# The row-sum test and its second path at the program's end, attention by halves of the channels, and the first convolution tile prepared in the last attention unit

## The chip, the cores and the metric

The kernel runs on one core of a Trainium2 chip. The metric is the device time of one execution in microseconds (us). PE is TensorE (matmuls), DVE is VectorE, ACT is ScalarE, POOL is GpSimd; SP issues most of the loads, ACT and POOL issue the stores. A core has 16 DMA engines which serve all of these queues. PSUM is the buffer into which matmuls write, in banks of 128 x 512 fp32 numbers.

## The reference

A network of four layers on x of 4 images x 256 channels x 64 x 64, each as x + layer(groupnorm(x)) with 32 groups. Only the first two layers and the start of the third matter here:

```
x = x + _L0(_gn(x))      # attention along each image row, 16 groups
x = x + _L1(_gn(x))      # 3x3 convolution with ternary weights
x = x + _L2(_gn(x))      # two grouped 3x3 convolutions of signs, batch norms
x = x + _L3(_gn(x))      # 3x3 convolution with computed weights

# _L0, for each image row n and group g:
qkv = batchnorm(einsum('nci,oc->noi', x, w_qkv));  q, k, v = split(qkv)
qe = einsum('ngci,cij->ngij', q, q_emb);  ke = the same with k, k_emb
qk = einsum('ngki,ngkj->ngij', qe, ke)
sim = softmax(sum of batchnorm([qk, qe, ke]), over j)
attn   = einsum('ngij,ngcj->ngci', sim, v)       # "values"
attn_e = einsum('ngij,cij->ngci', sim, v_emb)    # "embedded"
out = batchnorm([attn, attn_e]) summed in pairs  # the third batch norm
```

The softmax subtracts the row's maximum. The kernel first computes it without the subtraction, notes whether all row sums stay between 1e-20 and 1e20, and has a second path with the subtraction in case they do not. With these inputs they do, and the second path does not run.

## The kernel before

The whole program is one stream of instructions per engine. Most of the order on each engine comes from the order of the program text; a scheduler may move instructions, except where `tc.high_priority()` raises a block or `tc.keep_in_program_order` pins one. Buffers come from pools: a pool's slots are reused, and an instruction that writes a reused slot waits for the last reader of it. Pools grow from the left or the right side of the memory (`side="right"`).

The stages by the trace: normalisation and qkv product up to 285 us; scores qk into the DRAM buffer qk_d up to 970 (L471 to L599); attention up to 1558; the ternary convolution "d" in Winograd form from 1586 to 2111 (L1000, tiles named dc); the two binary convolutions, "e" (L1237, tiles pc), up to 2407; the last convolution "g" (L1000 again, tiles gc) up to 2941; then the last output store.

**Attention** works in 8 units (b, th): image b and half th of the channels, ordered with th inside b. A unit has 8 steps k of its scores: `scores` loads 1 MB of qk into one of three buffers si (L746) and a q tile (qc, L725, scaled on ACT at L734), makes the relative term by matmul (L757) and adds both on DVE into pt (L767); `exponentials` run on ACT (L797); `sums` are matmuls into den (L808). `reciprocals` inverts den on DVE (L817), lets POOL multiply the range test into the tile `good` (L821, L822), and spreads the result through PE and ACT to rb (L826, L828). Then come 8 `values` (L835) with `values_out` (product with rb L844, bn_stats L849, 256 KB store to at_d[0] by ACT's queue L850, two buffers o0), and 8 `embedded` (L859, product L865) into one 2 MB tile o1, with `next_scores` of the next unit after each. `embedded_out` ends the unit with 8 bn_stats (L874) and one 2 MB store to at_d[1] (L875).

The last unit stops after its reciprocals. Then comes the test: minimum of good over the row (L923), scaling (L924), a matmul (L926), a cast to an integer (L928), and a branch that every engine reads (L930). Behind it `last_unit` does the embedded part first, then the values.

**The norm of the attention's output** is `value_norm(th, two)` (L938 to L957): bn_aggr over the statistics of all images, a square root on ACT (L102, which needs another table than the exponentials), some operations on single columns, a small matmul (L955, pprm).

**Convolution d**: `prepare(b, t)` builds a tile of 128 channels t of the input: `load_1` loads x (dx<-in_x), then for two = 1 and then 0 and 8 pieces each loads a piece of at_d[two] (128 x 512, two issues on SP per piece, two buffers a per value of two) and adds it scaled to x on DVE (L1174); on the second pass DVE takes bn_stats of the sum (L1178). `norm` finds the group norm (matmuls pst, L111 to L122, square root, L1092 and L1181), `transform(b, t, h)` scales half an image on ACT into a padded tile (L1114, L1118) and makes 12 DVE operations of Winograd's input transform (L975 to L986, tile dtr). `rest` runs the 16 chunks (b, h, co): 36 matmuls each into six PSUM banks out of a ring of seven, then the output transform on DVE (L1020 to L1035), the store of x. For the first chunk, `first` = (0, 1): all products of t=0 are made before those of t=1. In program order the first tile is prepared so:

```
set_up()
with tc.high_priority():
    prepare(0, 0)
for t in range(2):
    load_weights(t, nc.sync)
norm(0, slice(0, 1))
transform(0, 0, 0)
prepare(0, 1)
norm(0, slice(1, 2))
transform(0, 1, 0)
for t in range(2):
    transform(0, t, 1)
rest()
```

Of the kernel before, what the change touches and what calls it, by code (L numbers as in the profile page):

```python
# [9 lines left out]
F32 = mybir.dt.float32  # L10
# [7 lines left out]
P = 128  # L18
B = 4
# [21 lines left out]
def network(ctx: ExitStack, tc, x, wqkv, relm, relt, relw, relv, counts, masks, vecs, rowv, ab, w1, l2w1, l2w2, l3w, mats, out):  # L41
# [15 lines left out]
    qk_d = [scratch(f"qk_d{b}", [GP, P, HW]) for b in range(B)]  # L57
    at_d = [[scratch(f"at_d{two}{b}", [C, HW]) for b in range(B)] for two in range(2)]
# [39 lines left out]
    def inv_std(pool, var, eps, shape):  # L98

        t = small(pool, shape)  # L100
        nc.vector.tensor_scalar(t, var, eps, None, ALU.add)
        nc.scalar.activation(t, t, AF.Sqrt)  # L102
        r = small(pool, shape)
        nc.vector.reciprocal(r, t)
        return r
# [560 lines left out]
    cph = ctx.enter_context(ExitStack())  # L666
    cp = pool(cph, "c", side="right")
    st3 = cp.tile([P, 2, 2, B * NB, 6], F32, name="st3")
    qp, ip = cqp, cip
    rp = pool(cph, "c_r")  # L670
    pp = pool(cph, "c_p")
    op = pool(cph, "c_o")
    cp_ = pool(cph, "c_e")
    wp = pool(cph, "c_w", 2)
    pse = pool(cph, "c_pse", 2, PSUM)
    psn = pool(cph, "c_psn", 1, PSUM)
    pso = pool(cph, "c_pso", 3, PSUM)

    vb = [rp.tile([P, 2, 4, 32, 8], F32, name=f"vb{m}") for m in range(4)]
    for m in range(4):  # L680
        nc.gpsimd.memset(vb[m], 0.0)

    pt = pp.tile([P, 32, 4 * 64 * 2 + 16], F32, name="pt")[:, :, 0 : 4 * 64 * 2].rearrange(
        "p i (a n b) -> p i a n b", a=4, b=2
    )
    rb = pp.tile([P, 32, 64, 2], F32, name="rb")

    rw = cp_.tile([P, 127, 2], F32, name="rw")
    nc.sync.dma_start(out=rw, in_=relw)

    ve = cp_.tile([P, W, 32], F32, name="ve")
    nc.gpsimd.memset(ve, 0.0)
    for r in range(2):
        src = bass.AP(tensor=relv.tensor, offset=relv.offset, ap=[[16, 64], [16, 64], [1, 16]])
        nc.sync.dma_start(out=ve[r:P:2, :, 16 * r : 16 * r + 16], in_=src)
    cnt = cp_.tile([P, 16, 32 + P], F32, name="cnt")
    nc.sync.dma_start(out=cnt, in_=counts)
    ones, pick = cnt[:, :, 0:32], cnt[:, :, 32 : 32 + P]
    units = [(b, th) for b in range(B) for th in range(2)]

    def attention(general, good):

        scale_e = se if general else seq

        def load_values(u, m):
            b, th = units[u]
            for r in range(2):
                for h in range(2):  # L710
                    nc.sync.dma_start(
                        out=vb[m][r:P:2, h, :, 16 * r : 16 * r + 16, :]
                        .rearrange("p a c m -> p a (c m)"),
                        in_=vt_d[b][m, r, 64 * h : 64 * h + 64, 4 * th : 4 * th + 4]
                        .rearrange("p a c m -> p a (c m)"),
                    )

        qts = {}

        def terms(u, m):  # L720

            b, th = units[u]
            q = qp.tile([P, 4, 2, 2, 64], F32, name=f"qc_{b}_{th}_{m}_{general}", tag="qc")
            for par in range(2):
                nc.sync.dma_start(  # L725
                    out=q[:, :, par].rearrange("p a k n -> p a (k n)"),
                    in_=q_d[b].rearrange("a (two k) t r c f -> two (k t r c) a f", two=2)[par][
                        :, 4 * th : 4 * th + 4, bass.ts(m, P)
                    ],
                )  # L730
            for a in range(4):
                gp = 4 * th + a
                qf = q[:, a].rearrange("p x k n -> p (x k n)")
                nc.scalar.activation(  # L734
                    qf, qf, AF.Identity, bias=scale_e[:, 1, gp : gp + 1], scale=scale_e[:, 0, gp : gp + 1]
                )
            qts[u, m] = q

        def scores(u, k):

            b, th = units[u]
            if k % 2 == 0:
                terms(u, k // 2)
            q = qts[u, k // 2]
            si = ip.tile([P, 4, 4, P], F32, name=f"si_{b}_{th}_{k}_{general}", tag="si")
            nc.sync.dma_start(  # L746
                out=si.rearrange("p a i f -> p a (i f)"),
                in_=qk_d[b][4 * th : 4 * th + 4].rearrange("a p f -> p a f")[:, :, bass.ts(k, 512)],
            )
            es = [  # L750
                pse.tile([P, 2, 4, 64, 2], F32, name=f"e_{b}_{th}_{k}_{y}_{general}", tag="e") for y in range(2)
            ]
            for par in range(2):
                for x_ in range(4):
                    rows = slice(32 * x_, 32 * x_ + 32)
                    i = 8 * k + 2 * x_ + par
# [4 lines left out]
            for y in range(2):  # L761
# [4 lines left out]
                if not general:  # L766
                    nc.vector.tensor_tensor(dst, e, src, ALU.add)  # L767
                    continue
# [874 lines left out]
```

## Time and profile before

| | |
|---|---|
| time, median of 3 runs | 2950.59 us (2935.45 to 2956.39) |
| the profiled execution | 2953.15 us, its span 2951.4 us |
| PE busy | 2599.9 us, 88% of the span |
| DVE busy | 2063.2 us, 70% |
| ACT busy | 1040.3 us, 35% |
| DMA, mean | 164 GB/s |
| an ordinary attention unit | about 71 us |
| cast of the count, next PE matmul | 1507.24, 1512.14 us |
| last values product ready, first dc matmul | 1558.45 (its DVE product), 1586.05 us |
| dc matmuls without a gap from | 1625.90 us |
| last output store issued, end of span | 2943.53, 2951.4 us |

A line of the timeline has the start and the duration in us, the engine, the line of the kernel, the operation, what it writes and reads, how many instructions are drawn together, and in brackets the idle time of the engine before it and what ended that. "<-issue" means that the profile shows nothing that the engine waited for. The table of stretches gives the busy time of each engine between two times, then the mean clock granted to PE (1 is full), the mean busy share of the DMA engines and what they moved in GB/s.

### The profile page before, as it was taken

What the parts mean: (1) busy time and instruction counts of PE and PEld (TensorE: products, weight loads), DVE (VectorE), ACT (ScalarE), POOL (GpSimd) and SP (SyncE); (2) the same over time, 40 slices, a digit from 0 to 9 for tenths busy, and PEclk for the clock granted to TensorE, in tenths of its full rate; (3) what the DMA queues carried; (4) which work ended last, traced back from release to release, by engine and by line L of the source; (5) the groups of instructions that cost most, each with busy time, mean ns of one, the idle gap of its engine ahead of it and who ended that gap; (6) DMA issues with size and microseconds to landing.
All of it is one profiled execution on the core that took longest, in us unless ns stands there. A gap on an engine that the chain in (4) does not pass through costs nothing. (4 is left out here: it accounts for less than half of the span.)

```text
span 2951.4 us, 77589 instructions
## 1 busy us (share of the span) xinstructions
PE 2599.9 (88%) x34248; PEld 1592.9 (54%) x34248; DVE 2063.2 (70%) x3653; ACT 1040.3 (35%) x1993; POOL 79.3 (3%) x153
## 2 busy tenths in 40 slices
PE   7999889899899787778763999999996978999998
PEld 4666556677677566666652444444454533444443
DVE  6555997666666465556557898985788978859642
ACT  4554445555455644445420010111246821101100
POOL 0000000000000100000000000000000000000000
PEclk9999999999999799988986999999998988999999
DMA  6767465555454777778747435322335663333201
GB/s 236 261 212 218 134 190 141 140 142 134 118 137 101 224 246 242 245 242 265 238 171 236 143 100 176 116 93 94 118 129 196 246 251 114 118 132 111 89 29 43
DMA packets 246806, 484.64 MB, mean 164 GB/s; under 512 B 28672, under 2 KB 128640, under 8 KB 220608
## 3 DMA queue, kind: packets, MB, share of 16 engines
q1 hardware_dynamic: 182304, 294.13, 31.1%
q10 hardware_dynamic: 54880, 125.84, 15.1%
q0 software_dynamic: 9280, 59.64, 5.1%
q8 instruction: 271, 4.44, 0.6%
q14 instruction: 71, 0.58, 0.1%
HBM read 283.20 MB, written 196.35 MB: 162 GB/s over the span
## 5 line engine op out<-in xcount | busy, mean ns | idle before, releaser
L1000 PE MATMUL dc<-dtr,d_u 128*128 128x512 f32 x1152 | 504.2, 598 | 16.9 <-DVE dtr L986 11.5
L1000 PE MATMUL gc<-gtr,g_u 128*128 128x512 f32 x1152 | 505.2, 600 | 14.8 <-DVE pc_o L1249 10.2
L478 DVE STREAM_TRANSPOSE t<-pd 128x1024 f32<-128x1024 f32 x256 | 304.0, 1226 | 113.9 <-PE pd L471 113.9
L1000 PEld LDWEIGHTS gc<-gtr,g_u 128*128 128x128 f32 x1152 | 219.8, 192 | 291.4 <-issue 271.4
L1000 PEld LDWEIGHTS dc<-dtr,d_u 128*128 128x128 f32 x1152 | 218.1, 191 | 287.4 <-issue 264.6
L471 PE MATMUL pd<-rm,qb 64*32 64x256 f32 x8192 | 286.4, 387 | 49.9 <-DVE t L478 43.0
L490 PEld LDWEIGHTS pq<-t,t 64*64 64x64 f32 x8192 | 260.1, 136 | 72.7 <-issue 49.8
L490 PE MATMUL pq<-t,t 64*64 64x64 f32 x8192 | 279.9, 221 | 18.6 <-issue 16.9
L1237 PE MATMUL pc<-e_tr,e_k 128*64 128x512 bf16 x2304 | 260.0, 385 | 19.0 <-DVE e_tr L1227 14.9
L494 ACT ACTIVATE o<-pq 128x512 f32<-128x512 f32 x256 | 152.4, 596 | 320.1 <-PE pq L490 320.0
L797 ACT ACTIVATE pt<-pt,sm 128x512 f32<-128x512 f32 x256 | 163.0, 709 | 198.2 <-DVE pt L767 198.1
L471 PEld LDWEIGHTS pd<-rm,qb 64*32 64x32 f32 x8192 | 156.4, 108 | 135.1 <-DVE t L478 61.9
L1237 PEld LDWEIGHTS <-e_k 128*64 128x64 bf16 x2304 | 141.2, 110 | 134.3 <-issue 21.5
L767 DVE TENSOR_TENSOR pt<-e_False,si_False 128x1024 f32<-128x1024 f32 x128 | 151.5, 1218 | 38.9 <-PE e_False L757 37.8
L499 ACT ACTIVATE pq<-pq 128x512 f32<-128x512 f32 x256 | 149.8, 585 | 3.9
L757 PE MATMUL e_False<-qc_False,rw 32*128 32x256 f32 x1024 | 124.5, 470 | 22.8 <-DVE pt L767 14.2
L1018 ACT COPY gc_c<-gc 128x512 f32<-128x512 f32 x32 | 18.6, 581 | 335.5 <-PE gc L1000 335.5
L835 PE MATMUL pa_False<-pt,vb 128*32 128x64 f32 x4096 | 101.8, 244 | 35.2 <-issue 22.0
L1018 ACT COPY dc_c<-dc 128x512 f32<-128x512 f32 x32 | 18.6, 582 | 321.2 <-PE dc L1000 306.3
L279 PE MATMUL po<-xg,wt 128*128 128x512 f32 x256 | 121.2, 613 | 7.1 <-DVE st L286 5.5
L859 PE MATMUL pe_False<-pt,ve 128*32 128x64 f32 x4096 | 88.8, 239 | 40.9 <-issue 29.8
L294 PE MATMUL pv<-wt,xg 128*128 128x256 f32 x512 | 122.2, 388 | 0.0
(395 smaller groups left out, 3371.1 us busy)
## 6 DMA issues: line engine op xcount, KB each, us to landing
si_False<-qk_d SPq DMA_DIRECT2D x64, 1024.0 KB
qk_d<-o ACTq DMA_DIRECT2D x124, 512.0 KB
x<-x_d SPq DMA_DIRECT2D x32, 1056.0 KB
a<-at_d SPq DMA_DIRECT2D x256, 128.0 KB
xa<-in_x SPq DMA_DIRECT2D x16, 1024.0 KB
vt_d<-vs ACTq DMA_DIRECT2D x32, 512.0 KB
q_d<-qs SPq DMA_DIRECT2D x64, 256.0 KB
qb<-q_d SPq DMA_DIRECT2D x128, 128.0 KB
```

The source lines that it names most:

```text
L279: nc.tensor.matmul(psf, lhsT=wt[:, t, bass.ts(o, P)], rhs=xg[:, t, :], start=(t == 0), stop=(t == 1))
L294: nc.tensor.matmul(pv[:, j, :], lhsT=xg[:, t, pix], rhs=wt[:, t, C : 2 * C], start=(t == 0), stop=(t == 1),)
L471: nc.tensor.matmul(pds[t][32 * c : 32 * c + 32, m].rearrange("p j k -> p (j k)"), lhsT=q[rows, 2 * (gp % 2) + g, a, 32 * nb : 32 * nb + 32 ...
L478: nc.vector.transpose(ts[t][:, :, 32 * jh : 32 * jh + 32].rearrange("p a j b -> p j a b"), pds[t].rearrange("p m j k -> p j m k"),)
L490: nc.tensor.matmul(ps[rows, m, :], lhsT=ts[1][rows, n // 2, :, n % 2], rhs=ts[0][rows, n // 2, :, n % 2], start=True, stop=True, tile_posi ...
L494: nc.scalar.activation(o[:, :, 8 * k : 8 * k + 8, :], ps.rearrange("p n (a b) -> p a n b", b=2), AF.Copy, accum_out=acc[:, 0, gp, col : co ...
L499: nc.scalar.activation(psf, psf, AF.Square, accum_out=acc[:, 1, gp, col : col + 1])
L757: nc.tensor.matmul(es[x_ // 2][:, x_ % 2, :, :, par], lhsT=rw[rows, 63 - i : 127 - i].rearrange("p j r -> p (j r)"), rhs=q[rows, :, par, k ...
L767: nc.vector.tensor_tensor(dst, e, src, ALU.add)
L797: nc.scalar.activation(s, s, AF.Exp, scale=s2q[:, gp : gp + 1])
L1000: nc.tensor.matmul(ms[k], lhsT=u[:, t, dx, k, bass.ts(co, P)], rhs=vs[t][:, k, :, dx : dx + 64], start=(first and dx == 0), stop=(last and ...
L1237: nc.tensor.matmul(m[64 * g : 64 * g + 64], lhsT=parts[:, g, i, k, dx, :], rhs=vs[g][:, k, 8 * (q % 2) : 8 * (q % 2) + 8, dx : dx + 64], s ...
```

## The change

All that follows the scores becomes a function `from_scores(general, keep)`, and the second path is a second call of it: the minimum of `good` is kept in `bad`, and the test (scaling, matmul, cast, branch) stands after the last convolution; if it fails, everything from the attention on is computed once more.

The units run with b inside th, so that th=0 is done for all images after the fourth unit; its two value norms are computed in the fifth (`u == B`), with a PSUM tile of the pool pso. The last unit runs like the others, values and then embedded.

The embedded output leaves in quarters: o1 is 128 x 1024 in two buffers, and after each odd k two bn_stats and a 512 KB store follow. at_d[1] is stored in the quarters' order, and `load_1` reads it by strided views. `load_1` now takes two = 0 first; its a buffers alternate by q (four in all); for image 0 the sum comes from the add itself (accum_out) and the sum of squares from an ACT Square into the spare padded tile, with `whole_stats` to finish, while for the other images four bn_stats follow each half.

The order of the first tile's preparation changes, the weights of d are two tiles loaded at different places, the pools of d, e and g are laid out anew (for d the ring of seven PSUM banks is four banks and three banks of two pools), the row-sum matmul takes its ones as a window of a smaller constant, and `inv_std` takes max(., 0) along with its addition. The diff, without changes of indentation and cut to its core (`value_norm` moves unchanged except for its last argument):

```diff
@@ -101 +102 @@
-        nc.vector.tensor_scalar(t, var, eps, None, ALU.add)
+        nc.vector.tensor_scalar(t, var, eps, 0.0, ALU.add, ALU.max)
@@ -665,0 +667,2 @@
+    def from_scores(general, keep):
+
@@ -668,0 +672,4 @@
+        if general:
+            ip = pool(cih, "c_i", 3)
+            qp = pool(cih, "c_q", 3)
+        else:
@@ -671,6 +678,3 @@
-    pp = pool(cph, "c_p")
-    op = pool(cph, "c_o")
-    cp_ = pool(cph, "c_e")
-    wp = pool(cph, "c_w", 2)
-    pse = pool(cph, "c_pse", 2, PSUM)
-    psn = pool(cph, "c_psn", 1, PSUM)
+        cp_ = pool(cph, "c_e", side="right")
+        wp = pool(cph, "c_w", 2, side="right")
+        pp = pool(cph, "c_p", side="right")
@@ -677,0 +682,2 @@
+        psn = pool(cph, "c_psn", 1, PSUM)
+        pse = pool(cph, "c_pse", 2, PSUM)
...
@@ -698,2 +704,2 @@
-    ones, pick = cnt[:, :, 0:32], cnt[:, :, 32 : 32 + P]
-    units = [(b, th) for b in range(B) for th in range(2)]
+        pick = cnt[:, 62:].rearrange("p (s m) -> p s m", s=16)
+        units = [(b, th) for th in range(2) for b in range(B)]
@@ -701 +707,27 @@
-    def attention(general, good):
+        prs = {}
+
+        def value_norm(th, two, psp, tag):
+
+
...
@@ -852 +885 @@
-        o1s = {}
+            o1s = [None]
...
@@ -863,2 +897,3 @@
-            if k == 0:
-                o1s[u] = op.tile([P, 64, 32, 2], F32, name=f"o1_{u}_{general}", tag="o1")
+                if k % 2 == 0:
+                    o1s[0] = wp.tile([P, 64, 8, 2], F32, name=f"o1_{u}_{k}_{general}", tag="o1")
+                o = o1s[0]
@@ -866 +901 @@
-                o1s[u][:, :, 4 * k : 4 * k + 4, :], ps.rearrange("p a n b -> p n a b"),
+                    o[:, :, bass.ts(k % 2, 4), :], ps.rearrange("p a n b -> p n a b"),
@@ -869,7 +904,5 @@
-
-        def embedded_out(u):
-            b, th = units[u]
-            of = o1s[u].rearrange("p n a b -> p (n a b)")
-            for k in range(NB):
-                nc.vector.bn_stats(st3[:, th, 1, b * NB + k, :], of[:, bass.ts(k, 512)])
-            nc.scalar.dma_start(out=at_d[1][b][bass.ts(th, P), :], in_=of)
+                if k % 2 == 1:
+                    of = o.rearrange("p n a b -> p (n a b)")
+                    for h in range(2):
+                        nc.vector.bn_stats(st3[:, th, 1, b * NB + k - h, :], of[:, bass.ts(h, 512)])
+                    nc.scalar.dma_start(out=at_d[1][b][bass.ts(th, P), bass.ts(k // 2, 1024)], in_=of)
@@ -894,3 +926,0 @@
-            if u + 1 == len(units):
-                reciprocals(u, 1)
-                break
@@ -901 +931 @@
-                if k % 2 == 1:
+                    if k % 2 == 1 and u + 1 < len(units):
@@ -902,0 +933,3 @@
+                if u == B:
+                    for two in range(2):
+                        prs[0, two] = value_norm(0, two, pso, "o")
@@ -904,0 +938 @@
+                    if u + 1 < len(units):
@@ -906,11 +939,0 @@
-            embedded_out(u)
-
-        def last_unit():
-            u = len(units) - 1
-            for k in range(NB):
-                embedded(u, k)
-            embedded_out(u)
-            for k in range(NB):
-                values_out(u, k, values(u, k))
-
-        return last_unit
@@ -921,2 +944,2 @@
-    last_unit = attention(False, good)
-    bad = small(cp, [P, 1])
+        attention(general, good)
+        bad = small(keep, [P, 1])
@@ -924,35 +946,0 @@
-    nc.vector.tensor_scalar(bad, bad, -float(P), float(P), ALU.mult, ALU.add)
-    ps = pso.tile([P, 1], F32, name="pbad", tag="o")
-    nc.tensor.matmul(ps[0:1], lhsT=bad, rhs=mt[:, M_ALL, 0:1], start=True, stop=True)
-    count = cp.tile([1, 1], mybir.dt.int32, name="count")
-    nc.vector.tensor_copy(count, ps[0:1])
-    lost = nc.values_load(count[0:1, 0:1], min_val=0, max_val=P)
-    with tc.If(lost > 0):
-        attention(True, None)
-    last_unit()
-
...
@@ -1049,5 +1047,2 @@
-        ap_ = pool(ph, f"{name}_a", 2)
-        xslots = {k: pool(ph, f"{name}_x{k}") for k in x_order}
-        if name == "g":
-            op = pool(ph, f"{name}_o", 2)
-        wp = pool(ph, f"{name}_w")
+            ps_ = {k: pool(ph, f"{name}_{k}", 2 if k in ("a", "o") else 1) for k in layout.split()}
+            ap_, op, sp = ps_["a"], ps_["o"], ps_["s"]
@@ -1055,4 +1050,4 @@
-            op = pool(ph, f"{name}_o", 2)
-        tslots = {k: pool(ph, f"{name}_t{k}") for k in tr_order}
-        padp = pool(ph, f"{name}_p")
-        sp = pool(ph, f"{name}_s")
+                ring = [pool(ph, "d_ps", 3, PSUM)] * 3
+                pst = pool(ph, "d_pst", 1, PSUM)
+                ring = [pool(ph, "d_ps4", 4, PSUM)] * 4 + ring
+            else:
...
@@ -1165 +1161 @@
-            for two in (1, 0):
+                for two in range(2):
@@ -1167 +1163,2 @@
-                    prs[t, two] = value_norm(t, two, pst)
+                        if t == 1:
+                            prs[t, two] = value_norm(t, two, pst, "pst")
@@ -1170,4 +1167,14 @@
-                        part = bass.ts(4 * half + q, HW // 8)
-                        cols = bass.ts(q, HW // 8)
-                        a = ap_.tile([P, HW // 8], F32, name=f"a_{b}_{t}_{half}_{q}_{two}", tag=f"a{two}")
-                        load_shuffled(a, at_d[two][b][bass.ts(t, P), part], 0, 64)
+                            k = 4 * half + q
+                            a = ap_.tile([P, HW // 8], F32, name=f"a_{b}_{t}_{half}_{q}_{two}", tag=f"a{q % 2}")
+                            if two == 0:
+                                load_shuffled(a, at_d[0][b][bass.ts(t, P), bass.ts(k, HW // 8)], 0, 64)
+                                xv = xh[half][:, bass.ts(q, HW // 8)]
+                                av = a
+                            else:
+
+                                load_shuffled(
+                                    a, at_d[1][b][bass.ts(t, P), q * 1024 + half * 512 : q * 1024 + half * 512 + 512], 0, 64
+                                )
+                                xv = xh[half].rearrange("p (n i) -> p n i", i=64)[:, :, bass.ts(q, 16)]
+                                av = a.rearrange("p (n i) -> p n i", i=16)
+                            kw = {"accum_out": st[:, k, 0:1]} if b == 0 and two == 1 else {}
@@ -1175 +1182 @@
-                            xh[half][:, cols], a, prs[t, two][:, 0:1], xh[half][:, cols], ALU.mult, ALU.add
+                                xv, av, prs[t, two][:, 0:1], xv, ALU.mult, ALU.add, **kw
@@ -1177,2 +1184,8 @@
-                        if two == 0:
-                            nc.vector.bn_stats(st[:, 4 * half + q, :], xh[half][:, cols])
+                            if kw:
+                                cols = slice(16 * q, 16 * q + 16)
+                                nc.scalar.activation(
+                                    spare[:, 1:33, 1 + 16 * q : 17 + 16 * q], xh[half].rearrange("p (n i) -> p n i", i=64)[:, :, cols],
+                                    AF.Square, accum_out=st[:, k, 1:2],
+                                )
+                        if two == 1 and b > 0:
+                            half_stats(st, half, xh[half])
@@ -1179,0 +1193 @@
+                    whole_stats(sp, mv, st)
@@ -1182 +1196 @@
-            return shift[t], False
+                return shift[t], b == 0
@@ -1199 +1213 @@
-            "d", ph, u1_d, (0, 1, 3, 5, 2, 4), (2, 3, 0, 1, 4, 5), M_GRPS, load_1,
+                "d", ph, u1_d, "x0 a p0 x1 t0 u0 x2 x3 s u1 o x4 t2 t3 t1 x5 t4 t5 p1", M_GRPS, load_1,
@@ -1203 +1216,0 @@
-        with tc.high_priority():
@@ -1205,2 +1218,2 @@
-        for t in range(2):
-            load_weights(t, nc.sync)
+            load_weights(0, nc.sync)
+            with tc.high_priority():
@@ -1209,0 +1223 @@
+            load_weights(1, nc.sync)
@@ -1213 +1227 @@
-            transform(0, t, 1)
+                transform(0, t, 1, True)
...
@@ -1265,4 +1280,5 @@
-        tslots = {k: pool(ph, f"e_t{k}") for k in range(4)}
-        wp1 = pool(ph, "e_w1")
-        tslots.update({k: pool(ph, f"e_t{k}") for k in (4, 5)})
-        padq = pool(ph, "e_q")
+            tslots = {k: pool(ph, f"e_t{k}") for k in (0, 1)}
+            tslots[5] = pool(ph, "e_t5", side="right")
+            padq = pool(ph, "e_q", side="right")
+            wp1 = pool(ph, "e_w1", side="right")
+            tslots.update({k: pool(ph, f"e_t{k}", side="right") for k in (3, 2, 4)})
...
@@ -1532,0 +1547,18 @@
+        return bad
+
+    bad = from_scores(False, keep)
+
+    with ExitStack() as ph:
+        sp = pool(ph, "z_s")
+        far = small(sp, [P, 1])
+        nc.vector.tensor_scalar(far, bad, -float(P), float(P), ALU.mult, ALU.add)
+        count = sp.tile([1, 1], mybir.dt.int32, name="count")
+        with ExitStack() as sums:
+            psp = pool(sums, "z_ps", 1, PSUM)
+            ps = psp.tile([P, 1], F32, name="pbad", tag="pbad")
+            nc.tensor.matmul(ps[0:1], lhsT=far, rhs=mt[:, M_ALL, 0:1], start=True, stop=True)
+            nc.vector.tensor_copy(count, ps[0:1])
+        lost = nc.values_load(count[0:1, 0:1], min_val=0, max_val=P)
+        with tc.If(lost > 0):
+            with ExitStack() as again:
+                from_scores(True, pool(again, "z_keep"))
...
```

## The prediction

> **What bounds the kernel now.** I read the page's engine shares first, then the busy table by stretch around the attention's end, then the timeline of TensorE (PE) there, then one ordinary attention unit in the same views, then the waits. PE is the bound over the whole program (88%), so only stretches in which PE is idle can pay.
>
> ```profile
> PE 2599.9 (88%) x34248; PEld 1592.9 (54%) x34248; DVE 2063.2 (70%) x3653; ACT 1040.3 (35%) x1993; POOL 79.3 (3%) x153
> 1500.00:1520.00 20.00, 10.79 (x195) 9.28 (x194) 6.10 (x21) 3.92 (x6) 1.98 (x4) 0.78 0.32 106
> 1520.00:1540.00 20.00, 10.59 (x515) 9.87 (x518) 12.77 (x22) 0.00 (x0) 0.00 (x0) 0.90 0.44 171
> 1540.00:1560.00 20.00, 10.07 (x384) 9.34 (x384) 15.55 (x26) 0.20 (x1) 0.00 (x0) 0.76 0.78 233
> 1560.00:1580.00 20.00, 2.77 (x10) 2.43 (x10) 15.70 (x65) 5.15 (x6) 0.00 (x0) 0.50 0.91 337
> 1580.00:1600.00 20.00, 13.95 (x27) 6.09 (x28) 17.59 (x28) 0.00 (x0) 0.00 (x0) 0.73 0.37 124
> 1600.00:1625.00 25.00, 8.23 (x22) 4.07 (x20) 15.05 (x30) 3.56 (x4) 0.00 (x0) 0.72 0.71 220
> ```
>
> The columns are length, PE, weight loads, DVE, ACT, POOL, granted clock, DMA share, GB/s. Of these 125 us PE works 56.4, while DVE works 82.8: here the chain of DVE and DMA, not PE, is the bound. The timeline says what PE waits for:
>
> ```profile
> 1507.24 0.15 DVE L928 CAST count<-pbad 1x1 int32<-1x1 f32 x1 [1.24 <-PE pbad L926]
> 1512.14 0.43 PE L859 MATMUL pe_False<-pt,ve 128*32 128x64 f32 x6 [4.94 <-PEq L930]
> ...
> 1586.05 20.58 PE L1000 MATMUL dc<-dtr,d_u 128*128 128x512 f32 x42 [11.48 <-DVE dtr L986]
> 1618.64 0.59 PE L111 MATMUL pst<-sm,mt 128*128 128x1 f32 x2 [12.01 <-DVE sm L1092]
> 1625.90 24.56 PE L1000 MATMUL dc<-dtr,d_u 128*128 128x512 f32 x50 [5.42 <-DVE dtr L979]
> ```
>
> The branch holds PE 4.94 us; the first convolution's products start at 1586.05 and starve between 1606.6 and 1625.9, because the second half of the tile (t=1) is added, measured and transformed late. From 1625.9 PE runs without a gap. An ordinary unit (1398 to 1438) is different:
>
> ```profile
> 1398.00:1406.00 8.00, 7.44 (x225) 5.94 (x223) 6.00 (x6) 5.77 (x11) 0.00 (x0) 0.90 0.99 317
> 1406.00:1414.00 8.00, 5.79 (x195) 4.73 (x189) 4.83 (x5) 7.67 (x14) 0.00 (x0) 1.00 1.05 352
> 1408.18 0.75 PE L859 MATMUL pe_False<-pt,ve 128*32 128x64 f32 x37
> 1411.14 0.66 PE L859 MATMUL pe_False<-pt,ve 128*32 128x64 f32 x27 [2.21 <-issue]
> 1425.66 2.47 DVE L874 BATCH_NORM_STATS2 st<-o_False 128x6 f32<-128x512 f32 x4
> DVE o_False L844 <- DMA at_d<-o_False: 31.5, 22, 2.9
> ```
>
> While one unit's embedded products and the next unit's scores run, the DMA engines are full (share 1.05 at 352 GB/s), and PE stops in the middle of a group of 64 equal matmuls for "issue".
>
> **What the skill says.** The Trainium skill, "Runtime: NRT & Kernel Launch", Instruction fetch mechanics: code streams in by DMA in 16 KiB blocks, and a taken branch out of the window stalls on such a fetch. The trace agrees: queue 8, "instruction", moved 4.44 MB in 271 packets (16.4 KB each), and the branch cost PE 4.94 us and DVE 4.05. That the mid-group stops are late blocks behind full DMA engines is my reading. "DMA: Bandwidth & Descriptors", Issuing engines are not separate DMA queues: ACT's stores and SP's loads share the 16 engines, so a store moved among loads competes with them. "ScalarE: Activation LUTs", What ACT_TABLE_LOAD costs: about 1.28 us plus a drain, 2.66 us a switch; the trace has the 1.28 at 1510.90. "TensorE: Matmul & The Clock Gate", HAM clock gate: an idle PE falls to half clock; the 1560 to 1580 stretch shows 0.50, so a shorter gap also brings fuller clock.
>
> **The change part by part.**
>
> Test moved to the end. Removed at 1507: the minimum, scale, matmul, cast and branch, 4.94 us on PE. Added after the last gx add (DVE, 2942.54 + 0.69): one 0.15 us cast before that add, then a register load and a branch on each engine, by the old place about 4.9 us, to 2948.1. The last output store issued at 2943.53 ends the span at 2951.4, so 7.3 us of landing cover it: I take +1, from 0 to +5 if the branch serialises behind POOL's store.
>
> Last unit and first tile. Before: embedded part, then values, then the sums of t=0 with 8 of its 16 adds left. After: values first; the adds of t=0 (128x512, 0.73 to 0.75 us each) go between values and embedded work, where DVE is idle. Values are paced by their stores, 5.2 us a pair (four pairs): from 1508 to about 1526. Embedded, eight groups at about 1.55 us of DVE (0.69 product, 0.69 statistics, a share of the adds): consumed by 1538. Then the rest of t=0 (six adds at the old cadence of 1.3 us, 8), two aggregates (2.0), a table load (1.28) and the short chain of th=1's value norm (2.2, an estimate from the like chain at 1513): 1551.5. On SP's queue the three loads of the first weights now stand ahead of the second set of pieces for t=0 and wait for the last values product on PE, which ends before 1526, so I count no more than the cadence above. Statistics from accumulators and ACT squares replace 16 bn_stats (16 x 0.62 = 9.9 us off DVE; ACT is nearly idle here). Short sum 1.2 and norm chain 4.6 (1570.36 to 1574.99 before): pad at 1558, transform of 12 DVE operations at 0.62 us interleaved with the t=1 adds: products start at 1566 to 1570 instead of 1586. For t=1, 16 adds are 12 us of DVE, but two issues of 0.5 to 0.6 us per piece and landings of 2.6 to 3.3 set about 1585; norm, pad and three transform operations (10.5) restart PE at 1595 instead of 1625.9, 31 us earlier. Not all of it stays: in the new order the transform of the other half (11 x 0.62 = 6.8 us) stands between these and the output adds, which free the PSUM banks. Four plus three banks cover one chunk; the third chunk starts about 1624 to 1626 where it was about 1650. I book -26, bounds -14 (landings stretch, as 337 GB/s at 1560 to 1580 allows) and -36 (no hold by the outputs).
>
> Order of the units and th=0's norm. The same loads and products, only (b, th) exchanged. The norm's square roots now fall among exponentials in unit 4: two switches each way of 1.28 us, 5.5 with their waits, on an ACT which has slack: +2 (0 to +5.5). Two small matmuls follow work long done.
>
> Embedded output by quarters. Eight bn_stats per unit leave the unit's end (2.47 us ahead of the last score adds, at 1425.66) for two after each odd group (1.23 each). Where DVE waits for PE, as at 1411, that gains up to 2.5 us a unit; where DVE is full (3.05 of 3.2 us a step around 1475) it costs 4 x 1.23 - 2.47 = 2.4. I take 0, bounds -17 to +17 over 7 units. The 2 MB store at 1425.66 becomes four of 512 KB, three of them inside the full stretch: 1.5 MB at 352 GB/s is 4.3 us a unit if all of it displaces loads. In 1398 to 1425 about 8.1 MB moved where 352 GB/s would carry 9.5, so 1.4 MB of room exists. I take +1 a unit, +7, from 0 to +30. The three extra issues stand on ACT's queue (0.33 us each) ahead of the next exponentials and wait there for DVE's odd product; ACT waited for DVE at those places anyway (1.15 and 2.23 us), so they cost nothing more unless ACT falls behind.
>
> Convolution d onwards. The ring of 4+3 banks is the same count. At the end of d, three norm matmuls now precede the first product of e; before, 33 of those products (3.6 to 3.8 us) ran at 2111.46 while the statistics came: +3.7, with nothing else on PE to hide it. Loads in e keep order with one exchange: +1 (0 to +3).
>
> Sum against the profiled execution (2953.15 us, span 2951.4): -26 +2 +0 +7 +3.7 +1 +1 = -11.3, so 2941.9. It lies 2.6 above the median of 2950.59; the same difference from the median gives 2939.3. I predict 2939.
>
> **Rivals.** (1) The whole boundary is won: -36, no contention, +3.7 in e, others 0: -32, 2918. For it: DVE has 42 us of idle in the 125; against it: the transforms ahead of the outputs. (2) The gain is eaten on DVE in attention: statistics ahead of score adds, 2.4 x 7 = 17: +6, 2956. For it the full DVE at 1475; against it that 1394 to 1430 shows DVE waiting. (3) Slower: the quarter stores meet full DMA engines in the embedded stretch and delay PE's code. Price: one more stop of 2.3 us for each of four stores in 7 units, 64 instead of the 7 booked: -11 + 57 = +46, 2996. It makes the kernel slower than before from 2.6 us a unit (18.3 / 7), and by over 1% from 6.8. For it: share 1.05 and stops of 2.2 to 2.4 us; against: si loads were waited for only 1.0 us in all. That the change does not do what it says I exclude: the new order has the adds of t=0 in the last unit and the test last.
>
> **Chances.** Forecast 0.45, rival 1 0.25, rival 2 0.18, rival 3 0.12. A change under 1% (29.5 us) can't be told from none by this measurement. Faster by over 1%: rival 1 and 0.02 of the forecast's early edge, 0.27; slower: rival 3, 0.12; within 1%: 0.61. The range 2908 to 2970 holds the forecast's bounds, rivals 1 and 2, and leaves out rival 3 and a tail below.
>
> **What would show it.** Right: no gap at the old branch, first dc product by 1570, restart near 1595 on the old clock, three pst matmuls ahead of the first pc product with some 4 us of idle PE, out store to end unchanged. Wrong: units of attention longer than 71 us with more "issue" before pe matmuls (rival 3) or DVE score adds behind bn_stats (rival 2); a restart after 1610; or more than 8 us between the last out store and the end.

## The result and the profile after

Over 20 runs of each, the changed kernel's median is 2945.26 us (2936.19 to 2958.24) against 2949.8 us (2935.45 to 2966.72): a ratio of 0.9986, with a 95% interval from 0.9969 to 1.0002. That is about 4 us less, and as the interval includes 1, 20 runs can't tell it from nothing. The two profiled executions are 2953.15 and 2940.49 us, 12.7 apart; each lies on its own side of its median (3.4 above, 4.8 below), so the ledger below is about 8 us kinder to the change than the medians are.

The boundary first. The busy table of the changed kernel, with the same columns (length, PE, weight loads, DVE, ACT, POOL, clock, DMA share, GB/s):

```profile
1500.00:1520.00 20.00, 15.44 (x635) 14.22 (x627) 12.88 (x22) 2.04 (x2) 1.98 (x4) 1.00 0.65 216
1540.00:1560.00 20.00, 2.77 (x10) 2.43 (x10) 14.30 (x60) 11.06 (x23) 0.00 (x0) 0.52 0.60 181
1580.00:1600.00 20.00, 14.31 (x32) 6.54 (x31) 12.00 (x32) 4.35 (x9) 0.00 (x0) 0.83 0.63 243
1600.00:1625.00 25.00, 25.00 (x59) 10.96 (x58) 24.86 (x41) 3.91 (x5) 0.63 (x1) 1.00 0.05 13
```

PE's quiet stretch (2.77 of 20 us) has moved from 1560 to 1580 to 1540 to 1560, and from 1600 on PE is full. Of ACT's 11.06 us in the quiet stretch the squares are 5.76. PE's timeline there, then at the start of e and before the second convolution of e, and last the same two places in the kernel before:

```profile
1565.80 21.14 PE L989 MATMUL dc<-dtr,d_u 128*128 128x512 f32 x42 [9.61 <-issue]
1593.51 46.71 PE L989 MATMUL dc<-dtr,d_u 128*128 128x512 f32 x102 [5.44 <-DVE dtr L967]
...
2084.92 0.59 PE L112 MATMUL pst<-mv,mt 128*128 128x2 f32 x2 [6.89 <-DVE mv L1206]
2086.70 28.60 PE L1251 MATMUL pc<-e_tr,e_k 128*64 128x512 bf16 x244
...
2228.51 1.01 PE L1420 MATMUL psg<-sm,mt 64*128 64x4 f32 x4 [10.28 <-DVE sg L1422]
...
2111.46 3.24 PE L1237 MATMUL pc<-e_tr,e_k 128*64 128x512 bf16 x27
2250.11 1.01 PE L1401 MATMUL psg<-sm,mt 64*128 64x4 f32 x4 [5.49 <-DVE sg L1403]
```

The branch's gap is gone, the first product of d is 20.3 us earlier, the restart 32.4 us. Then gains are given back: PE waits 6.89 us in front of d's last norm, where before it worked on e, and 10.28 us before the second group of psg matmuls, where it waited 5.49 before.

Read as lengths between marks, in us (the "last rb copy" ends the row sums of unit 8; "restart" is the dc product after which PE has no gap):

| stretch | before | after | booked | difference |
|---|---|---|---|---|
| first e matmul of attention to last rb copy | 521.8 | 521.5 | +9 | -0.3 |
| last rb copy to first dc product | 77.9 | 59.2 | | -18.7 |
| first dc product to restart | 39.9 | 27.7 | | -12.2 |
| restart to end of d's products | 485.6 | 484.5 | | -1.1 |
| (the three rows above) | | | -26 | -32.0 |
| end of d to second convolution of e | 154.5 | 166.4 | +4.7 | +11.9 |
| from there to the last output store | 677.5 | 679.6 | 0 | +2.1 |
| last output store to end of span | 7.8 | 14.5 | +1 | +6.7 |

With 1.3 us at the start of attention these add up, but for rounding, to the difference of the spans, 12.8. The row before the last, +2.1, was not pursued. What the last row is, the instructions of the engines' sequencers say (POOLq is POOL's: it waits, branches and issues). Of the changed kernel (engine, operation, count: shortest/median/longest in ns, first and last start), POOL's instructions of the branch and of the program's end, and then those of the kernel before:

```profile
2924.09 0.53 POOL L1527 DMA_DIRECT2D out<-gx  x1 [30.37 <-DVE gx L1024]
L1562 POOLq EVENT_SEMAPHORE  x5: 17/43/5110, 2925.1 to 2930.5; - x5
L1562 POOLq INC_SWDGE_SEM  x1: 1547/1547/1547, 2930.6 to 2930.6; - x1
L1671 POOLq DRAIN  x3: 40/107/5623, 2932.2 to 2938.3; - x3
...
L1639 POOLq DRAIN  x3: 40/113/7013, 2943.5 to 2951.1; - x3
```

Before, POOL drains for 7.0 us while its store lands. After, the end of the branch makes POOL wait 5.1 us for the landing, count up its semaphores for 1.5 us, and only then drain, for 5.6 us more.

### The profile page after: what moved, and what is told of

It reads as the page before. It is cut to its first block, busy times and chain, and to the rows that moved or that the text cites. A ratio compares the mean times of both kernels' runs of the same rounds, so it can differ in the third digit from the quotient of the medians.

```text
span 2938.6 us, 77718 instructions
## 1 busy us (share of the span) xinstructions
PE 2603.1 (89%) x34248; PEld 1599.4 (54%) x34248; DVE 2050.6 (70%) x3661; ACT 1055.2 (36%) x2029; POOL 79.1 (3%) x153
## 4 chain that ended last, share of the span: by engine, by line
PE 27%; issue 22%; DVE 7%; DMA 6%; ACT 3%; POOL 0%; SPq 0%; ACTq 0%; POOLq 0%; DVEq 0%
PE dc L989 15%; PE pc L1251 4%; DMA at_d<-o_False 3%; PE e_False L790 2%; PE den_False L841 2%; DVE pt L800 2%; PE pe_False L893 2%; DMA qc_False<-q_d 1%; PE pr_False L859 1%; PE pa_False L868 1%; ACT pt L830 1%; DVE o_False L877 1%; DMA x<-x_d 1%; ACT e_pad L1468 1%; ACT rb L861 1%
## 5 line engine op out<-in xcount | busy, mean ns | idle before, releaser
L491 PE MATMUL pq<-t,t 64*64 64x64 f32 x8192 | 278.4, 220 | 17.5 <-issue 15.6
L1251 PEld LDWEIGHTS <-e_k 128*64 128x64 bf16 x2304 | 144.8, 111 | 134.0 <-issue 24.7
L295 PEld LDWEIGHTS pv<-wt,xg 128*128 128x128 f32 x512 | 96.5, 191 | 33.4 <-issue 19.2
```

Source lines behind the costliest of these rows:

```text
L295: nc.tensor.matmul(pv[:, j, :], lhsT=xg[:, t, pix], rhs=wt[:, t, C : 2 * C], start=(t == 0), stop=(t == 1),)
L491: nc.tensor.matmul(ps[rows, m, :], lhsT=ts[1][rows, n // 2, :, n % 2], rhs=ts[0][rows, n // 2, :, n % 2], start=True, stop=True, tile_posi ...
L1251: nc.tensor.matmul(m[64 * g : 64 * g + 64], lhsT=parts[:, g, i, k, dx, :], rhs=vs[g][:, k, 8 * (q % 2) : 8 * (q % 2) + 8, dx : dx + 64], s ...
```

## The experiments

Every run below is one profiled execution, except the last, and is read by lengths between its marks: the 20 whole times of the kernel before lie anywhere between 2935 and 2967 us.

**The test at the end, left out.**

```diff
-    with ExitStack() as ph:
-        sp = pool(ph, "z_s")
...
-                from_scores(True, pool(again, "z_keep"))
```

> The changed kernel without the test and the second path at its end (left out: the fallback that recomputes everything). From the last output store's issue to the end of the span: 7.9 us in the kernel before, 14.5 in the changed one. Theory 'POOL's waits fall in series' (at the branch POOL first waits for its store to land, then clears, then drains for 5.6 us): without the branch the stretch is 7.5 to 8.5 us, so the end costs about 6.6. Theory of the prediction (the landing covers the branch, 0 to 5, about 1): 13 to 14.5 us. All other stages keep their marks (first dc product 1566, restart 1594, first pc product 2087, all within 3 us).

From the last store to the end it took 7.8 us (2924.63 to 2932.4), so the test at the end costs 6.7 us, not 1. The other marks stand 3 to 5 us later than expected, since attention took 527.9 us in this run; as lengths they are the same. The whole was 2934.17 us.

**Only the last output store on SP.**

```diff
-                nc.gpsimd.dma_start(out=out[b, bass.ts(co, P), bass.ts(h, HW // 2)], in_=xh)
+                eng = nc.sync if (b, h, co) == (B - 1, 1, 1) else nc.gpsimd
+                eng.dma_start(out=out[b, bass.ts(co, P), bass.ts(h, HW // 2)], in_=xh)
```

> The changed kernel with only its very last output store issued by SP instead of POOL; test and branch stay. Theory 'POOL's waits in series': POOL then has no late store to wait for at the branch and drains while SP's store lands: last store to end 8 to 10.5 us instead of 14.5. Rival 'the branch itself with its code fetch is what costs': 13 us or more.

It took 8.5 us (2926.93 to 2935.4). POOL's long drain in this run:

```profile
2926.93 0.35 SPq L1528 DMA_DIRECT2D out<-gx  x1
L1672 POOLq DRAIN  x3: 40/107/5542, 2929.0 to 2935.1; - x3
```

The drain takes 5.5 us as in the changed kernel, but starts at 2929.0, 2 us after the store's issue instead of 8. With its test the end now takes only 0.7 us more than in the run without one (8.5 against 7.8), so what cost was POOL's landing in front of POOL's drain. No run has SP's store and no test, so the 0.7 is not the price of the branch alone.

**Stage e's x tiles in one pool.**

```diff
-            xp3 = pool(ph, "e_x", 3)
+            xp_ = pool(ph, "e_x", 4)
...
-            xp1 = pool(ph, "e_x1")
...
-                xt = (xp1 if taken[0] % 4 == 3 else xp3).tile([P, 33, 64], F32, name=f"{name}_{b}_{t}_{h}", tag="x2")
+                xt = xp_.tile([P, 33, 64], F32, name=f"{name}_{b}_{t}_{h}", tag="x2")
```

> The changed kernel with stage e's x tiles in one pool of four buffers again, instead of three and one. It puts SP's loads of x in e back into the order of use. Theory 'the split pool let the scheduler put loads ahead that have to wait, and the last loads of the first binary convolution land late': the gap of PE before the second group of psg matmuls falls from 10.3 us to 5 to 6, and from the first gapless pc product to the second convolution's first takes 151 us as before (2115.2 to 2266.05) instead of 157.8; about 5 to 7 us less in all. Rival 'the loads are late because of the right-side pools or the bytes in flight': gap stays near 10 us. The three norm matmuls still stand ahead of the first pc product, with about 7 us of PE idle before them.

PE in this run, then ACT in the changed kernel, where the late load stood, and ACT at the same tile in this run:

```profile
2231.85 1.01 PE L1419 MATMUL psg<-sm,mt 64*128 64x4 f32 x4 [5.49 <-DVE sg L1421]
...
2218.17 4.31 ACT L1468 ACTIVATE e_pad<-x,sm,sm 64x2112 bf16<-64x2112 f32 x2 [4.60 <-DMA x<-x_d]
2223.68 0.58 ACT L1259 COPY pc_o<-pc 128x512 f32<-128x512 f32 x1
...
2213.02 2.15 ACT L1467 ACTIVATE e_pad<-x,sm,sm 64x2112 bf16<-64x2112 f32 x1 [0.62 <-DMA x<-x_d]
```

The gap is 5.49 us again, and from the first pc product to the second convolution it takes 151.1 us. In the changed kernel ACT waited 4.60 us for an x tile and only then copied the last pc product, on which the end of the first convolution depends; with one pool it waited 0.62. That the split pool let later loads move ahead on SP's queue fits this, but the views don't tell the single x tiles apart, so it is not shown. From d's end to the second convolution it takes 159.7 us, against 161.5 to 166.4 (mean 164.1) in the seven versions that have d's PSUM and e's pools as the changed kernel: 4.4 less. Part of it is lost again later: from the second convolution to the last store this run takes 681.4 us, the seven 678.4 to 679.6.

**Stage d's PSUM in one ring.**

```diff
-                ring = [pool(ph, "d_ps", 3, PSUM)] * 3
-                pst = pool(ph, "d_pst", 1, PSUM)
-                ring = [pool(ph, "d_ps4", 4, PSUM)] * 4 + ring
+                pst = pool(ph, "d_pst", 1, PSUM)
+                ring = [pool(ph, "d_ps", 7, PSUM)]
```

> The changed kernel with stage d's PSUM as before: the norm's bank first and one ring of seven banks, instead of rings of four and three. It puts the first 33 pc products ahead of d's last norm matmuls on PE. Theory 'the split ring moved the bank that e takes first and with it the order': PE starts e right after d's last product, and 3.6 to 5 us are won there; the boundary of attention and d keeps its marks (first dc product 1566, restart 1594, within 3 us), since attention's banks are free before. Rival 'the split ring is what lets d start early': first dc product 5 us or more later, or a gap in the first chunks.

```profile
2080.44 4.77 PE L1250 MATMUL pc<-e_tr,e_k 128*64 128x512 bf16 x41
2087.41 0.38 PE L112 MATMUL pst<-mv,mt 128*128 128x2 f32 x2 [2.20 <-DVE mv L1205]
```

PE works on e for 4.77 us in front of the norm. From d's end to the second convolution it takes 160.3 us, 3.8 less than the mean above. The edit restores both the one ring and the place of the norm's bank; which of the two moves the order was not tried. First product and restart of d come 60.1 and 84.8 us after the last rb copy (59.2 and 86.9 in the changed kernel): the split ring was not what let d start early.

**The kernel before without its test.**

```diff
-    lost = nc.values_load(count[0:1, 0:1], min_val=0, max_val=P)
-    with tc.If(lost > 0):
-        attention(True, None)
     last_unit()
```

(the matmul and the cast in front of it go too)

> The kernel before without the test and the second path in its middle (left out: the fallback). Theory of the prediction: PE's gap of 4.9 us goes and the chain of DVE and DMA behind it moves up by the same: first dc product about 1581, restart about 1621, 5 us less in all. Rival 'the chain is bound by the landing of the pieces, not by the branch': restart stays within 2 us of 1625.9. Rival 'the branch also held up the loads and the scheduler': restart at 1610 or earlier.

The first product came 57.5 us after the last rb copy and the restart 97.4 (77.9 and 117.7 before): 20.3 us for a gap of 4.9, as the last rival said. The time was 2921.0 us, one run, but below every run of the kernel before (the lowest of all is 2924.07). PE around the last rb matmuls (L826) in this run, then SP's first loads of d's x in the kernel before and in this run:

```profile
1487.40 2.63 PE L859 MATMUL pe_False<-pt,ve 128*32 128x64 f32 x97 [2.13 <-DVE o_False L865]
1492.59 3.84 PE L826 MATMUL pr_False<-rd_False,cnt 128*128 128x128 f32 x32 [0.30 <-DVE rd_False L817]
...
1512.06 3.21 SPq L142 DMA_DIRECT2D dx<-in_x  x4
...
1462.72 10.97 SPq L142 DMA_DIRECT2D dx<-in_x  x5
```

Embedded matmuls of the last unit stand in front of and among the row sums. SP's first load of d stood 3.9 us behind the last rb copy (1508.2) and now stands 34.8 us ahead of it (1497.5), and the first matmul of the value norms comes with that copy (1497.3), where it came 10.5 us behind it.

**The branch with an empty second path.**

```diff
     with tc.If(lost > 0):
-        attention(True, None)
+        nc.vector.memset(good, 0.0)
```

> The kernel before with its test, count and branch, but with a second path that only clears one tile (left out: the fallback). In the earlier run without any test the time from the last rb copy to the restart of dc was 97.4 us instead of 117.7, 20 less, although PE's gap at the branch is only 4.9. Theory 'the wall': it is the second path, which writes pt, rb, vb and the outputs, that keeps every instruction of the last unit and of the first tile behind the branch; with nothing to protect, the branch may stand among the values, and the stretch is 96 to 104 us with the branch's 4 to 5 us somewhere in it. Rival 'the branch and its code fetch': 115 to 119 us.

102.4 us from the last rb copy to the restart (67.4 and 35.0). SP's first load of d stands 33.2 us ahead of the last rb copy. The branch is there, but it now stands among the values. PE behind it, the branch instructions of PE (here PEldq) and DVE in this run, and PE's in the kernel before:

```profile
1534.11 1.95 PE L835 MATMUL pa_False<-pt,vb 128*32 128x64 f32 x64 [5.48 <-DVEq L930]
L930 PEldq COMPARE_BRANCH  x1: 231/231/231, 1528.4 to 1528.4; - x1
L930 DVEq COMPARE_BRANCH  x1: 76/76/76, 1532.4 to 1532.4; - x1
...
L930 PEldq COMPARE_BRANCH  x1: 3806/3806/3806, 1508.0 to 1508.0; - x1
```

So about 15 of the 20 us go with the second path's body, and 5 stay with the branch (9.9 at the first product, of which 5 are made up by the restart). PE's gap is about as long as before but has another cause: before, PE's own branch instruction took 3.81 us; here it takes 0.23, and PE waits for DVE, which comes to the branch 4 us later. The shorter jump could thus account for up to 3.6 of the 15 us; the loads that now stand 37 us earlier can't come from it. Emptying the path removes what it reads as well as what it writes, and the two were not told apart.

**Quarters alone, in the kernel before.** In `embedded`, o1 becomes [P, 4, 64, 8, 2], and the statistics and the store follow each odd k; `load_1` reads as in the changed kernel.

> The kernel before with the embedded output in quarters: two bn_stats and a 512 KB store after each odd group, instead of eight and 2 MB at the unit's end; at_d[1] laid out and read accordingly; all else as before. The prediction booked +7 (0 to +30) for stores among loads and 0 (-17 to +17) for the statistics: the last rb copy of unit 8 at 1514 instead of 1507. Theory after the comparison of the two traces (attention as a whole ended 1.6 us earlier): quarters cost nothing, 1503 to 1509. Rival 'quarters gain and the order of the units loses': 1500 or earlier.

The last rb copy ended at 1498.7, in the range of the rival, but the mark can't decide: attention took 514.6 us, and in the three versions with the old attention 515.5 to 526.9. The two parts of a unit do move, against each other. From one rb copy to the next the long part (embedded products, most scores, five of eight groups of values) takes 52.4 us in the mean (50.5 before), the short part (the last row sums, three groups of values) 14.0 (16.5 before). All versions with quarters show it: 52.4 to 53.9 and 13.9 to 14.7, against 49.6 to 50.5 and 16.5 to 17.5 with the old attention. The stores and bn_stats slow the long part, into which they have moved, and free the short part. Which of the two does it is not shown: the edit moves both. Of the changed kernel (where the parts are 53.3 and 13.9), the stretch of the busy table in which DMA was at 1.05 and 352 GB/s before, and two of its waits:

```profile
1398.00:1406.00 8.00, 5.47 (x209) 4.58 (x208) 6.59 (x7) 5.24 (x10) 0.00 (x0) 1.00 1.06 379
1406.00:1414.00 8.00, 5.08 (x143) 4.18 (x135) 4.09 (x5) 5.32 (x11) 0.00 (x0) 0.82 1.07 375
ACT qc_False L767 <- DMA qc_False<-q_d: 47.0, 22, 4.2
PE pe_False L893 <- issue: 38.0, 21, 5.5
```

The waits for q tiles have about doubled: 37.7 to 48.9 us in all versions with quarters, 13.6 to 23.3 without. PE's "issue" before pe is 25.8 to 38.0 us with quarters, and 20.1 to 29.8 without; these ranges overlap.

**The order of the units.**

```diff
-        units = [(b, th) for th in range(2) for b in range(B)]
+        units = [(b, th) for b in range(B) for th in range(2)]
...
-                if u == B:
+                if u + 1 == len(units):
```

> The changed kernel with the units' order of before (th inside b); the norms of th=0 are then computed in the last unit, after its values, since th=0 ends with unit 7. Theory 'early norms of th=0 are what lets the first tile be added in the last unit': the adds of t=0 can't start before the norms, and the first dc product comes 4 to 10 us after 1566; the two square roots leave the exponentials. Rival 'the adds are paced by their loads, and the norms just need to be there before the values end': first dc product within 3 us of 1566, restart within 3 us of 1594.

First product 59.2 us after the last rb copy, restart 87.0: the same as in the changed kernel (59.2 and 86.9). Having the norms of th=0 early is worth nothing that these marks show. Attention took 521.6 us.

**Statistics on DVE.**

```diff
-                            kw = {"accum_out": st[:, k, 0:1]} if b == 0 and two == 1 else {}
+                            kw = {}
...
-                        if two == 1 and b > 0:
+                        if two == 1:
...
```

> The changed kernel with image 0's statistics by bn_stats on DVE (four after each half, then bn_aggr), as for the other images, instead of sums from the adds and squares on ACT. Theory 'DVE is the chain here': for t=0 and t=1 each, the last four bn_stats (2.5 us) and an aggregate stand between the last add and the norm, less the short sum of 1.2: first dc product 1568 to 1572, restart 1597 to 1602. Rival 'landings pace the adds and DVE has room': both marks within 2 us.

61.3 and 87.1 us, within what the other versions with the changed boundary show (59.1 to 61.8, and 84.8 to 87.6): the squares on ACT and the accumulators bring nothing that these marks show.

**The second half not pinned.**

```diff
-                transform(0, t, 1, True)
+                transform(0, t, 1)
```

> The changed kernel with the transforms of the second half, (0, t, 1), not pinned in the program's order. From the first dc product to its restart it takes 27.7 us in the changed kernel, 39.9 before and 40.0 before without the test; before, the 12 operations of the second half of t=0 (7.4 us) stand on DVE ahead of the adds of t=1. Theory 'the pinned order is what brings t=1 forward': 34 to 41 us. Rival 'the four buffers a': 26 to 29 us.

27.4 us from first product to restart (27.7 in the changed kernel): no effect.

**Two buffers a for each pass.**

```diff
-tag=f"a{q % 2}")
+tag=f"a{two}")
```

> The changed kernel with its a buffers named by two again, so that each of the two passes over a tile has two buffers instead of four. Theory 'the adds are paced by SP, two issues of 0.55 us per piece, and not by buffers': first dc product to restart 26 to 30 us. Rival 'two buffers hold back the loads': 33 us or more, and more of DVE's waits for a pieces.

28.2 us from first product to restart, as the theory said, but the first product came 64.7 us after the last rb copy, and the restart 92.9. The other nine versions with the changed boundary lie between 84.8 and 87.6, so the four buffers are worth about 6 us, ahead of the first product, where neither theory had looked. DVE's waits for pieces of a grew with it, as the rival had it: 27.4 us in all of d, 14.7 in the changed kernel.

**Four corrections together**: one pool for x, one ring, the last store on SP, the units' old order.

> The changed kernel with four corrections: e's x tiles in one pool of four, d's PSUM as one ring of seven with the norm's bank first, the very last store on SP, and the units in the order of before with the norms of th=0 in the last unit. If the parts add up (e 5, d to e 4.4, end 6, attention 0 to 4) it is 15 to 19 us faster than the changed kernel's median of 2945: 2926 to 2930, a ratio to the kernel before of 0.992 to 0.9935. If e's two corrections overlap or the attention's part was chance: 2930 to 2936, 0.9935 to 0.9955. If they cancel: above 0.997.

In five rounds the median was 2924.35 us (21 runs) against 2946.01 (26 runs) for the kernel before: a ratio of 0.994, interval 0.992 to 0.9959. The ratio stands for about 18 us less than before (12 to 24); the medians are 21.7 apart. The ratio thus lies in the second range of the expectation, the median below the first. The marks of its profiled execution: 87.4 us from the last rb copy to the restart, 155.2 from d's end to the second convolution (154.5 before), 8.5 at the end; attention took 525.7, so the old order of the units adds nothing. One pool and one ring took 4.4 and 3.8 us off the way to the second convolution, each alone, and take 8.9 together. Over the longer way from d's end to the last store each alone took only 2.2 and 3.3 off the seven's mean of 843.3 us, which is near their scatter (840.9 to 846.1), and together they take 11.0 (832.3; 832.0 before). Why they do more together was not pursued. With the 6.0 at the end (14.5 less 8.5) and the change's own 4 (0.6 more to 9 less, by its interval) one would expect 18 to 21, which is within the interval.

## Why the prediction was right or wrong

The measured 2945.26 us lies in the range of 2908 to 2970, 6 above the 2939 foretold, and "no change that can be told" was right. Part of this is luck, since errors cancelled: between the two profiles the boundary gave 6 us more than booked and attention cost 9 less, while e and the end cost 7 and 6 more than booked.

*The boundary, booked -26, was -32.0.* First product at 1566 to 1570 and restart at 1595 on the old clock were right: measured from the last rb copy they are at 1567.4 and 1595.1. The 5 us that I took off for the output transforms did not come: from the restart to the end of d it took 484.5 us against 485.6. The term that was mis-sized is the PSUM hold, which was none. Inside the timetable two errors cancelled. When the embedded products ended (1538.6), ten adds of t=0 were left, not six, but the aggregates, the table load and the value norm of th=1, booked as 5.5 us behind the adds, ran between them; the sum was complete at 1550.8, where I had 1551.5.

*Its parts were put down wrongly.* The branch was booked at its visible gap, 4.94 us. Taking out the test alone gives 20.3, and a branch with an empty second path costs only about 5 of them. Most of the cost was in what the second path uses, pt, rb, vb and the outputs among it: it holds the last unit and the first tile behind the branch, and a gap in the timeline doesn't show work that could have been done earlier. The 9.9 us off DVE by accumulators gave nothing that the marks show, and neither did early norms or the pinned order, each undone alone. Four buffers, not priced at all, give about 6, ahead of the first product. So of the 30.8 us from the last rb copy to the restart 20 go with the test, measured in the kernel before, and 6 with the buffers, measured in the changed one. Which edit gives the rest was not settled. The stretch from first product to restart, 39.9 us before and 40.0 without the test, is 24.7 to 28.2 in all ten versions with the changed boundary, so what brings t=1 forward by 12 us is none of the edits undone alone. The order of the two passes, the values before the embedded part, and the place of the weights' loads were not undone.

*Attention, booked +9, was -0.3 in the two profiles.* The contention was there, as rival 3 had it, but its other half was missing from the sum: what left the unit's end, bn_stats and store together, had slowed the short part, which gains some 2.6 us a unit where the long part loses 2 to 3. For the statistics alone the prediction had named such a gain, up to 2.5 us, and booked 0. Over the eight versions with the changed attention and the new order of units its length is 521.5 to 528.8 (mean 525.6), over three with the old attention 515.5 to 526.9 (mean 521.4); the old order of units gave 521.6 and 525.7. The means are 4 us apart and the ranges overlap: whether a few microseconds are lost there stays open.

*The start of e, booked +3.7, measured 3.8* by restoring d's PSUM layout: right in place and size, but the cause was the new layout, whose ring I had called neutral ("the same count").

*Loads in e, booked +1, measured 4.4* up to the second convolution. The step that failed is "loads in e keep order with one exchange": I saw the exchanges in the order and priced them by the slack in mid-stage; the end of the first convolution had none (ACT's wait there was 4.60 us, and 0.62 with one pool).

*The end, booked +1 (0 to 5), was 6.7.* The step that failed is "7.3 us of landing cover it". Landing and drain had run side by side on POOL; the branch put them one after the other. The sign named for this, more than 8 us from the last store to the end, is what showed it.

Rival 1 (-36 at the boundary) was 4 us off there, the forecast 6; rival 2 did not show; rival 3 showed its contention at a fraction of its price. The Trainium skill says in "Runtime: NRT & Kernel Launch", Instruction fetch mechanics, that a taken branch stalls on a fetch when its target is not among the pages already held. That fits PE's own branch instruction: 3.81 us over the long second path in the kernel before, 3.98 at the end of the changed program, 0.23 over the path of one instruction. No run isolates the fetch itself.

## What to carry to other kernels

A branch can cost more than its gap: the buffers that its body uses can hold back what stands behind it, up to 15 of 20 us here, so measure it by taking it out, or by emptying its body, before pricing its removal. At the end of a program ask what the last engine does after its last store, and give that store to a queue whose engine has nothing to drain. After any new layout of pools, compare the order of each queue and the first instructions of each stage, since a freed slot or bank changes what may be moved ahead.

## What the runs showed of the hardware

POOL's last drain took 5.5 to 5.6 us with nothing of POOL's left to land, and 7.0 us when its store's landing lay inside it; the instruction at the end of the branch that counts up POOL's semaphores took 1.5 us, behind the landing. PE's branch instruction took 3.81 and 3.98 us over a long body and 0.23 over a body of one instruction; ACT's, DVE's and POOL's took 0.05 to 0.08. In stretches of 8 us the DMA engines moved up to 372 GB/s before (1058 to 1066) and 379 in the changed kernel (1398 to 1406), at a share of 1.06 both times, above the 352 GB/s that I had taken as full.
